# A third expert matrix for narrow last tiles: partial products on groups of PSUM's partitions, added by one more product

## The chip, the cores and the metric

The kernel runs on one core of one Trainium2 chip, as one launch. The metric is the device time in microseconds. Before the change three runs took 674.23 to 675.20 us, with a median of 675.03 us.

## What is computed

The reference is one layer over `x` of 64 sequences with 32 rows of 256 values (2048 rows, called tokens below), all in fp32: a cross attention on a context of 257 rows per sequence, a local attention, and a mixture of experts. The change is in the last of the three:

```python
def _L0_ffn_ref(hidden_states, Wr, br, W1, b1, W2, b2, W3, b3):
    x = hidden_states.reshape(-1, d)
    router_logits = x @ Wr + br
    expert_mask = jax.nn.one_hot(jnp.argmax(router_logits, axis=-1), num_experts, dtype=x.dtype)
    out = jnp.zeros_like(x)
    for e in range(num_experts):
        h = jax.nn.gelu(x @ W1[e] + b1[e], approximate=False)
        h = jax.nn.gelu(h @ W2[e] + b2[e], approximate=False)
        y = h @ W3[e] + b3[e]
        out = out + expert_mask[:, e:e + 1] * y
    return out.reshape(b, s, d)
...
x = x + _L0_xattn_ref(_layernorm(x, axis=-1), ctx_768, mask_BxS2_bf1, ...)
x = x + _L0_attn_ref(_layernorm(x, axis=-1), ...)
x = x + _L0_ffn_ref(_layernorm(x, axis=-1), ...)
```

There are 8 experts; W1 is 256x1024, W2 is 1024x512, W3 is 512x256. Each token goes to one expert, the one with the largest router logit.

## The kernel before

**Phases.** Until about 430 us the kernel does both attentions, 32 pairs of sequences one after another, and routes the tokens: it numbers the tokens of each expert in a table and writes their normed and plain rows to a table in DRAM (`table_x`). From then on the expert stage runs, in pieces.

**Pieces.** A piece is up to 256 tokens of one expert. Each expert has one piece of its own; for all but the first expert it is made of 128 tokens (half h=0) and the expert's last, partly filled tile (half h=1), which has 0, 32, 64, 96 or 128 rows. How many is known only on the chip: `quarters(i)` loads the number of steps of 32, and a `tc.Switch` with five cases runs `piece(j, P + 32 * case)`. Between two experts' pieces may stand a "between" piece of 128 tokens, in a `tc.If`, for experts with more than two tiles. So all the code for n = 128, 160, 192, 224 and 256 is there in each Switch, and the data choose.

**What a piece does.** `piece` (L1291) is a fixed order on TensorE: `first` (L1237, first matrix, 256 to 1024, gelu on ScalarE at L1243), `second` in three calls (L1253, second matrix, 1024 to 512, gelu at L1264 into `h2`), in their midst `turn_next` (transposes of the next piece's tokens, L1113, into `y_ps[1]`, copied out by ScalarE at L1116), then `third`. In `first` and `second` the weights are the operand that is loaded (128 columns of it) and the n tokens move through, so their time grows with n. In `third` it is the other way round: a block of `h2`, 128 x rows, is loaded and a block of W3, 128 x 256, moves through. It takes four such products (c = 0 to 3) to sum over the 512 rows of W3, all into the same part of a PSUM bank; a half of 32 rows therefore needs the four products that a half of 128 rows needs.

**The order around it.** The program's order is kept as written on TensorE, VectorE, ScalarE and GpSimd (POOL). In `third`, for each half: POOL adds the bias to the plain rows (`xb`, L1270), TensorE makes four products (L1273) into `y_ps[h]`, VectorE adds the two (`y`, L1277), and POOL scatters `y` to the output with an indirect DMA (L1278). POOL does the first half's scatter before the second half's `xb`. The block c=3 of `h2` is the last one that ScalarE writes (L1264), just after TensorE has ended the second matrix.

**Weights.** Three sets of buffers (`ring`) are refilled by four DMAs on SP's queue per expert, wa (L955), bo (L956), wb (L957) and wc (L961), in that order, each as soon as the last reader of its buffer is done. `bo` is read by POOL's `xb`.

**Constants.** `_COLS` names column ranges of one packed input, `pack2`. Its first part (up to `qhead`) comes with one DMA (L603), the rest with another (L606), between the first and the second half of the first context block.

**PSUM.** The eight banks have fixed roles in the expert stage: three for the first matrix, three for the second, `y_ps[0]` and `y_ps[1]` for the third matrix's two halves; `y_ps[1]` also takes the transposes.

Of the kernel before, what the change touches and what calls it, by code (L numbers as in the profile page):

```python
# [7 lines left out]
F32 = mybir.dt.float32  # L8
# [10 lines left out]
P = 128  # L19
# [3 lines left out]
B, S, D = 64, 32, 256  # L23
M, CD = 257, 192
HEADS, HD = 16, 16
E, F1, F2 = 8, 1024, 512
# [17 lines left out]
for _name, _w in (  # L44
    ("ident", 128),
    ("qhead", 2),
    ("ones", 128),
    ("before", 128),
    ("band", 128),
    ("own", 2),  # L50
    ("rank", E),
    ("step", NT - 1),
    ("tile", NT - 1),
    ("after", NT - 1),
    ("queue", E),
    ("queue_tile", E),
    ("quarter", 4),
    ("upto", E * E),
    ("row", P),
    ("column", E * NT),  # L60
    ("token", NT),
    ("here", 1),
):
    _COLS[_name] = (_n, _n + _w)
    _n += _w
# [12 lines left out]
def constants():  # L78

    import numpy as np  # L80

    c = np.zeros((P, NCONST), np.float32)
    p = np.arange(P)

    def put(name, value):
        a, b = _COLS[name]
        c[:, a:b] = value

    put("ident", p[:, None] == p[None, :])
    put("ones", 1.0)  # L90
    put("before", p[:, None] < p[None, :])
    near = (p[:, None] // S == p[None, :] // S) & (abs(p[:, None] - p[None, :]) <= 2)
    put("band", np.where(near, 0.0, FMAX))
    own = (p[:, None] // HD) % 2 == np.arange(2)[None, :]
    put("qhead", np.where(own, HD**-0.5, 0.0))
    put("own", np.where(own, -1.0, 0.0))
    put("rank", E - np.arange(E)[None, :])
    put("step", P * np.arange(1, NT)[None, :])
    put("tile", np.arange(NT - 1)[None, :])
    put("after", np.arange(1, NT)[None, :])  # L100
    put("queue", T * np.arange(E)[None, :])
    put("quarter", 32 * np.arange(4)[None, :])
    put("queue_tile", NT * np.arange(E)[None, :])
    put("upto", (np.arange(E)[:, None] >= np.arange(E)[None, :]).reshape(1, -1))
    put("row", p[None, :])
    put("column", P * np.arange(E * NT)[None, :])

    put("token", P * np.arange(NT)[None, :] + p[:, None] - T)
    put("here", p[:, None])
    return c  # L110


@with_exitstack
def perceiver_layer_kernel(
# [14 lines left out]
    nc = tc.nc  # L129
# [17 lines left out]
    k_ = {name: v2["consts"][:, a:b] for name, (a, b) in _COLS.items()}  # L147
# [40 lines left out]
    def bank(name, shape=(512,)):  # L188
        n = 1
        for w in shape:  # L190
            n *= w
        t = psp.tile([P, 512], F32, name=name, tag="bank")[:, 0:n]
        return t if len(shape) == 1 else t.rearrange("p (a b) -> p a b", b=shape[1])
# [365 lines left out]
    with tc.tile_pool(name="xq", bufs=1) as qpool, tc.tile_pool(  # L559
        name="xin", bufs=2  # L560
    ) as inp, tc.tile_pool(name="xkv", bufs=3) as kvp, tc.tile_pool(
        name="xp", bufs=2
# [261 lines left out]
        ps = bank("vl")  # L824
# [143 lines left out]
    rp = ctx.enter_context(tc.tile_pool(name="rp", bufs=1))  # L968
# [3 lines left out]
    h1 = rp.tile([P, F1 // P, 2 * P], F32, name="h1")  # L972
    h2 = rp.tile([P, F2 // P, 2 * P], F32, name="h2")
    xb_of = [rp.tile([P, D], F32, name=f"xb{i}") for i in range(2)]
    y_of = [rp.tile([P, D], F32, name=f"y{i}") for i in range(2)]

    def gather_rows(dst, at):
# [82 lines left out]
    f1_ps, f2_ps, y_ps = banks[0:3], banks[3:6], banks[6:8]  # L1060
# [12 lines left out]
    def buffer_of(j):  # L1073

        kind, i = order[j]
        if kind != "between":
            return i % 2 if i > 0 else 2
        return 2 if i < E - 1 else (i - E + 1) % 3  # L1080
# [19 lines left out]
    def tokens_of(j, h):  # L1100
        if order[j][0] == "early":
            return token0
        at = halves(j)[h]
        return token[:, at : at + 1]
# [160 lines left out]

    def third(j, n):
        _, _, wc, bo = ring[buffer_of(j)]
        for h, rows in enumerate((P, n - P) if n > P else (P,)):
            xt, xb, y = xt_of[h][j % 3], xb_of[h][0:rows, :], y_of[h][0:rows, :]
            nc.gpsimd.tensor_tensor(xb, xt[0:rows, 1, :], bo[0:rows, :], ALU.add)  # L1270
            ps = y_ps[h][0:rows, 0:D]
            for c in range(F2 // P):
                nc.tensor.matmul(  # L1273
                    ps, h2[:, c, h * P : h * P + rows], wc[:, c, :],
                    start=c == 0, stop=c == F2 // P - 1,
                )
            nc.vector.tensor_tensor(y, ps, xb, ALU.add)  # L1277
            nc.gpsimd.indirect_dma_start(  # L1278
                out=out[:, :],
                out_offset=bass.IndirectOffsetOnAxis(ap=tokens_of(j, h)[0:rows, :], axis=0),  # L1280
                in_=y,
                in_offset=None,
                bounds_check=T - 1,
                oob_is_err=False,
            )
# [5 lines left out]
    def piece(j, n):  # L1291
        first(j, n)
        second(j, n, (0, 1))
        turn_next(j)
        second(j, n, (2,))
        second(j, n, (3,))
        third(j, n)
# [36 lines left out]
    rest_2(tableT, pick)  # L1334
    gather(2, 1)
    third(0, P)
    gather(3, 0)
    first(1, P)
# [5 lines left out]
    second(1, P, (2,))  # L1344
    second(1, P, (3,))
    third(1, P)
    fetch_at(3)
    for i in range(1, E):
# [26 lines left out]
def laid_out(inputs):  # L1375
# [24 lines left out]
    def pack(*parts):  # L1400
# [5 lines left out]
        "mask": a["mask_BxS2_bf1"].view(np.uint8),  # L1406
        "pack1": pack(ct[:, :, :, M - 1], wk, np.concatenate([wv, wv], axis=0)),
        "pack2": pack(halves(a["L0_xattn_Wq"]), constants()),
        "pack3": pack(
            halves(a["L0_xattn_Wo"]), halves(a["L0_attn_Wq"].T),  # L1410
# [30 lines left out]
```

## Time and profile before

| | |
|---|---|
| median of 3 runs | 675.03 us (674.23 to 675.20) |
| the profiled execution | 675.32 us; the span of its instructions 673.5 us |
| granted TensorE clock | 0.989 of full speed over the span |
| expert stage | from about 433 us to the end |
| third matrix, 128x256, one multiply | 0.379 us from start to modelled end, x136 |
| the same with 32 or 64 columns loaded | x16 and x8 |
| last gelu of a piece with 160 rows (L1264) | 0.39 us |
| addition of y (L1277), 128x256 from PSUM | 0.425 us |
| bias addition xb on POOL (L1270) | 0.74 us |
| scatter on POOL (L1278) | 1.0 us |

How to read it: the profile is of one execution, so sums from its rows are held against its own 675.32 us. Times in the views are microseconds from the start of the span. PE is TensorE's multiply, PEld its weight load, which runs beside multiplies. An fp32 product shows as two loads and two multiplies. A multiply's end is modelled, and multiplies overlap in the pipeline: what a row of them costs is read from start to start, not from their durations. "128*32 128x256" is a multiply with 128 rows and 32 columns loaded and 256 columns moving. In brackets stands the engine's idle time before a group and what ended it; "issue" is a wait for nothing that the profile shows.

### The profile page before, as it was taken

How to read it: one execution, taken by the hardware profiler on the slowest of the kernel's cores; microseconds unless marked ns; L12 is line 12 of the kernel's file. 1: busy time of each engine (PE TensorE's matmuls, PEld its weight loads, DVE VectorE, ACT ScalarE, POOL GpSimd, SP SyncE). 2: the span in 40 equal slices, each digit the busy share in tenths (PEclk: the TensorE clock that was granted, in tenths of full speed). 3: DMA queues.
4: the chain of work that ended last, by engine and by line, in shares of the span. 5: the costliest groups of instructions: out<-in, count | busy, mean ns of one | idle time of the engine just before them, and what ended most of it. 6: DMA issues, size and time to landing. Idle time of an engine off the chain costs nothing.

```text
span 673.5 us, 18635 instructions
## 1 busy us (share of the span) xinstructions
PE 643.5 (96%) x7033; PEld 535.0 (79%) x7033; DVE 320.2 (48%) x1211; ACT 341.0 (51%) x1052; POOL 343.6 (51%) x725
## 2 busy tenths in 40 slices
PE   5999999999999999999999986899999999999994
PEld 3777777777777777877877875899999999989894
DVE  3485776777876877777786883610000000000000
ACT  2865775585684775766766644433323222243220
POOL 1596585687588588578587561222313122331120
PEclk9999999999999999999999998799999999999998
DMA  8932213303313322221200019464794627961000
GB/s 295 309 104 104 65 42 103 103 10 127 104 27 111 103 63 82 97 83 61 97 34 2 3 50 385 177 253 153 254 318 141 210 91 235 347 224 41 27 17 27
DMA packets 23094, 85.51 MB, mean 127 GB/s; under 512 B 2465, under 2 KB 7842, under 8 KB 20208
## 3 DMA queue, kind: packets, MB, share of 16 engines
q1 hardware_dynamic: 19984, 74.64, 31.9%
q0 software_dynamic: 2912, 8.65, 4.0%
q8 instruction: 72, 1.18, 0.7%
q14 instruction: 126, 1.03, 0.5%
HBM read 103.64 MB, written 6.56 MB: 164 GB/s over the span
## 4 chain that ended last, share of the span: by engine, by line
PE 88%; DVE 4%; DMA 3%; issue 2%; ACT 1%; POOL 1%; SPq 0%; ACTq 0%; POOLq 0%
PE moe L1253 17%; PE k L651 13%; PE v L668 12%; PE moe L1237 9%; PE t L750 8%; PE s L684 5%; PE moe L1273 5%; PE pv L769 4%; PE wo L799 2%; PE q L582 2%; PE av L372 2%; PE am L355 2%; DMA xt<-table_x,token 2%; DMA ct<-in_ctxt 1%; PE as L399 1%
## 5 line engine op out<-in xcount | busy, mean ns | idle before, releaser
L711 ACT ACTIVATE p<-p,nmx 128x256 f32<-128x256 f32 x256 | 127.2, 499 | 69.0 <-DVE nmx L706 68.1
L737 POOL TENSOR_SCALAR p<-p,rd 128x256 f32<-128x256 f32 x256 | 117.1, 478 | 84.1 <-DVE rd L734 30.3
L1253 PE MATMUL moe<-h,wb 128*128 128x128 f32 (+3 forms) x992 | 128.9, 289 | 0.3 <-issue 0.3
L1253 PEld LDWEIGHTS moe<-h,wb 128*128 128x128 f32 x992 | 124.1, 192 | 2.0 <-issue 0.4
L1277 DVE TENSOR_TENSOR y<-moe,xb 128x256 f32<-128x256 f32 (+2 forms) x20 | 8.5, 423 | 216.1 <-PE moe L1273 193.0
L706 DVE CUSTOM_DVE_ANT_0 p<-s,mb 128x256 f32<-128x256 f32 x256 | 108.0, 478 | 3.8 <-PE s L684 3.8
L651 PE MATMUL k<-cp,pack 64*128 64x512 f32 x384 | 95.3, 618 | 0.9 <-POOL cp L637 0.9
L756 DVE COPY pt<-t 128x512 f32<-128x512 f32 x114 | 72.6, 674 | 49.3 <-PE t L750 49.3
L668 PEld LDWEIGHTS v<-pack,cp 64*128 64x128 f32 x768 | 78.9, 187 | 19.1 <-issue 8.6
L637 POOL TENSOR_SCALAR cp<-ct,pack 128x256 f32<-128x256 f32 x189 | 87.6, 479 | 11.8 <-DMA ct<-in_ctxt 10.2
L668 PE MATMUL v<-pack,cp 64*128 64x256 f32 x768 | 90.9, 377 | 0.0
L1278 POOL DMA_INDIRECT out_x<-y,token x20 | 20.0, 1002 | 127.1 <-DVE y L1277 105.8
L1264 ACT ACTIVATE h<-moe,wa 128x128 f32<-128x128 f32 (+3 forms) x64 | 23.2, 380 | 101.8 <-PE moe L1253 96.3
L1243 ACT ACTIVATE h<-moe,wa 128x128 f32<-128x128 f32 (+3 forms) x120 | 38.6, 379 | 63.6 <-PE moe L1237 59.7
L1237 PEld LDWEIGHTS moe<-xT,wa 128*128 128x128 f32 x480 | 60.3, 191 | 7.2 <-issue 5.0
L651 PEld LDWEIGHTS k<-cp,pack 64*128 64x128 f32 x384 | 39.3, 191 | 33.6 <-issue 25.3
L1237 PE MATMUL moe<-xT,wa 128*128 128x128 f32 (+3 forms) x480 | 63.8, 291 | 1.8 <-ACT h L1243 1.0
L750 PE MATMUL t<-pack,p 128*128 128x128 f32 x512 | 64.5, 277 | 0.2
L750 PEld LDWEIGHTS t<-pack,p 128*128 128x128 f32 x512 | 55.6, 141 | 10.9 <-issue 5.6
L711 ACT ACTIVATION_READ_ACCUMULATOR p<-p,nmx 128x1 f32 x256 | 48.5, 189 | 0.0
L978 POOL DMA_INDIRECT xt<-table_x,token x24 | 25.1, 1044 | 45.2 <-PE moe L1253 23.1
L769 PEld LDWEIGHTS pv<-pt,v 128*32 128x32 f32 x2048 | 30.2, 110 | 12.6 <-issue 4.6
(197 smaller groups left out, 835.4 us busy)
## 6 DMA issues: line engine op xcount, KB each, us to landing
wb<-in_WB SPq DMA_DIRECT2D x17, 2048.0 KB
ct<-in_ctxt SPq DMA_DIRECT2D x15, 1542.0 KB
wa<-in_WA SPq DMA_DIRECT2D x17, 1030.0 KB
wc<-in_WC SPq DMA_DIRECT2D x17, 512.0 KB
table_x<-aw SPq DMA_DIRECT2D x8, 512.0 KB
bo<-in_b SPq DMA_DIRECT2D x17, 128.0 KB
m<-in_mask SPq DMA_DIRECT2D x16, 128.5 KB
ct<-in_ctxt SPq DMA_DIRECT2D x2, 771.0 KB
```

The source lines that it names most:

```text
L637: engine.tensor_scalar(cp[:, r, j, :], loaded[b // BG][0][:, r, b % BG, 0:KL], -1.0, clast[:, r, b : b + 1], ALU.mult, ALU.add,)
L651: nc.tensor.matmul(ps[c], wk[h, r, :], cp[h, r, :, :].rearrange("p b k -> p (b k)"), start=r == 0, stop=r == 2,)
L668: nc.tensor.matmul(ps[t][:, j * D : (j + 1) * D], cp[h, r, j, t * P : (t + 1) * P], wv[h, r, :], start=r == 0, stop=r == 2,)
L706: nc.vector.tensor_tensor_reduce(out=p[:, j, i, :], in0=ps[i][:, j * KL : (j + 1) * KL], in1=mb[:, b % BG, 0:KL], scale=1.0, scalar=mb[:, ...
L711: nc.scalar.activation(p[:, j, i, :], p[:, j, i, :], AF.Exp, bias=nmx[:, j, i : i + 1], scale=-1.0, accum_out=sums[:, j, i : i + 1],)
L737: nc.gpsimd.tensor_scalar(p[:, j, i, :], p[:, j, i, :], rd[:, j, i : i + 1], 1.0, ALU.mult, ALU.mult)
L750: nc.tensor.transpose(ps[:, i * P : (i + 1) * P], prob[n][:, j, i, t * P : (t + 1) * P], ident)
L756: nc.vector.tensor_copy(pT[n][:, j, t, :], ps)
L769: nc.tensor.matmul(pv[32 * i : 32 * i + 32, c, j, :], v[:, t, j, at : at + 32], pt[:, j, t, i * P + 64 * c : i * P + 64 * c + 64], start=t ...
L1237: nc.tensor.matmul(ps[:, i, 0:n], wa[:, at : at + P], x_j[:, c, 0:n], start=c == 0, stop=c == 1,)
L1243: nc.scalar.activation(h1[:, f + i, 0:n], ps[:, i, 0:n], AF.Gelu, bias=wa[:, at : at + 1])
L1253: nc.tensor.matmul(pss[f], wb[:, c, f * P : (f + 1) * P], h1[:, c, 0:n], start=c == 0, stop=c == F1 // P - 1,)
```

## The change

A constant with columns `sum32` (1 where the partition's number modulo 32 equals the column) and one `sum64` (modulo 64) are added to the pack, 96 columns in all, and a tile `parts` of 128 x 256. If the last tile has 32 or 64 rows (`few`), `third` does that half differently. Before the first half, the four products for it are made, each onto its own group of 32 of `y_ps[1]`'s partitions (four groups), or, with 64 rows, onto two groups of 64, with two products summed in each. VectorE copies all 128 partitions to `parts`. When the second half's turn comes, one product with `sum32` or `sum64` as the loaded operand adds the groups up, into the next 256 columns of the same bank. For a last tile of 96 or 128 rows, and for pieces of 128, nothing changes. POOL's and VectorE's other work keeps its order.

```diff
+    ("sum32", 32),
+    ("sum64", 64),
...
+    put("sum32", p[:, None] % 32 == np.arange(32)[None, :])
+    put("sum64", p[:, None] % 64 == np.arange(64)[None, :])
...
+    parts = rp.tile([P, D], F32, name="parts")
...
     def third(j, n):
         _, _, wc, bo = ring[buffer_of(j)]
+        few = n - P if P < n <= P + 64 else 0
+        if few:
+
+            wide = 32 if few <= 32 else 64
+            ps = y_ps[1][:, 0:D]
+            for c in range(F2 // P):
+                at = c * wide % P
+                nc.tensor.matmul(
+                    ps[at : at + few, :], h2[:, c, P:n], wc[:, c, :],
+                    start=c * wide < P, stop=(c + P // wide) >= F2 // P,
+                )
+            nc.vector.tensor_copy(parts, ps)
         for h, rows in enumerate((P, n - P) if n > P else (P,)):
             xt, xb, y = xt_of[h][j % 3], xb_of[h][0:rows, :], y_of[h][0:rows, :]
             nc.gpsimd.tensor_tensor(xb, xt[0:rows, 1, :], bo[0:rows, :], ALU.add)
-            ps = y_ps[h][0:rows, 0:D]
-            for c in range(F2 // P):
+            if h and few:
+                ps = y_ps[1][0:rows, D : 2 * D]
                 nc.tensor.matmul(
-                    ps, h2[:, c, h * P : h * P + rows], wc[:, c, :],
-                    start=c == 0, stop=c == F2 // P - 1,
+                    ps, k_["sum32" if wide == 32 else "sum64"][:, 0:few], parts,
+                    start=True, stop=True,
                 )
+            else:
+                ps = y_ps[h][0:rows, 0:D]
+                for c in range(F2 // P):
+                    nc.tensor.matmul(
+                        ps, h2[:, c, h * P : h * P + rows], wc[:, c, :],
+                        start=c == 0, stop=c == F2 // P - 1,
+                    )
             nc.vector.tensor_tensor(y, ps, xb, ALU.add)
```

## The prediction

> **What bounds the kernel now.** I read the page first, then the chain of waits over the expert stage, then the one source line that the change rewrites, then the timeline around the pieces that it touches. The page:
>
> ```profile
> PE 643.5 (96%) x7033; PEld 535.0 (79%) x7033; DVE 320.2 (48%) x1211; ACT 341.0 (51%) x1052; POOL 343.6 (51%) x725
> ...
> PE 88%; DVE 4%; DMA 3%; issue 2%; ACT 1%; POOL 1%; SPq 0%; ACTq 0%; POOLq 0%
> ```
>
> TensorE is busy for 96% and carries 88% of the chain. The change sits in the expert stage; the chain there, from 430 us on, by line:
>
> ```profile
> by line: PE moe L1253 47.7%; PE moe L1237 24.4%; PE moe L1273 12.9%; issue 5.5%; PE moe L1113 2.0%; PE moe L1027 1.3%; PE table_ps L549 0.7%; POOL xt L978 0.4%; POOL out_x L1278 0.4%; POOL xb L1270 0.3%; ACT h L1243 0.2%; PE moe L1205 0.1%;
> ```
>
> So TensorE time in this stage is kernel time, and L1273, the third matrix, is on the chain. The view of that source line says how often the change applies:
>
> ```profile
> L1273 PEld LDWEIGHTS moe<-wc,h x160: 106/190/193, 439.1 to 663.8; 128*128 128x128 f32 x136, 128*32 128x32 f32 x16, 128*64 128x64 f32 x8
> L1273 PE MATMUL moe<-wc,h x160: 378/379/463, 439.1 to 664.0; 128*128 128x256 f32 x136, 128*32 128x256 f32 x16, 128*64 128x256 f32 x8
> ```
>
> A product in fp32 is two load-and-multiply pairs, and a half takes four products, so 8 pairs. 16 pairs of 32 columns are two halves of 32 rows, 8 of 64 columns are one of 64 rows. Three pieces of the run change; the other thirteen take the old code. The timeline around the first of them (third starts at 493.91):
>
> ```profile
> 493.91 3.73 PE L1273 MATMUL moe<-wc,h 128*128 128x256 f32 x16
> 494.17 0.39 ACT L1264 ACTIVATE h<-moe,wa 128x160 f32<-128x160 f32 x1 [1.78 <-PE moe L1253]
> 495.73 1.43 PEld L1273 LDWEIGHTS moe<-wc,h 128*32 128x32 f32 x8 [0.33 <-issue]
> 495.90 0.42 DVE L1277 TENSOR_TENSOR y<-moe,xb 128x256 f32<-128x256 f32 x1 [14.79 <-PE moe L1273]
> 496.60 1.03 POOL L1278 DMA_INDIRECT out_x<-y,token  x1 [8.15 <-DVE y L1277]
> 497.66 0.74 POOL L1270 TENSOR_TENSOR xb<-xt,bo 32x256 f32<-32x256 f32 x1
> ```
>
> Note the second line: the last gelu of h2 ends at 494.56, 0.65 us after TensorE has gone on to the third matrix. Today nothing waits: the product that needs it is the fourth of h=0. TensorE alone, for this piece, the 64-row one, and the 128-row one (which has no narrow tile):
>
> ```profile
> 493.91 3.73 PE L1273 MATMUL moe<-wc,h 128*128 128x256 f32 x16
> 497.58 3.84 PE L1237 MATMUL moe<-xT,wa 128*128 128x128 f32 x32
> 501.25 3.74 PE L1253 MATMUL moe<-h,wb 128*128 128x128 f32 x32
> ...
> 556.66 3.76 PE L1273 MATMUL moe<-wc,h 128*128 128x256 f32 x16
> 560.35 3.84 PE L1237 MATMUL moe<-xT,wa 128*128 128x128 f32 x32
> 564.03 3.74 PE L1253 MATMUL moe<-h,wb 128*128 128x128 f32 x32
> ...
> 648.09 3.62 PE L1273 MATMUL moe<-wc,h 128*128 128x256 f32 x16
> 651.54 3.73 PE L1237 MATMUL moe<-xT,wa 128*128 128x128 f32 x32
> 655.12 3.74 PE L1253 MATMUL moe<-h,wb 128*128 128x128 f32 x32
> ```
>
> From 648.09 to 651.54 are 16 pairs: 0.216 us each, and a narrow half costs as many. From the start of third to the start of the second matrix after it: 7.03 us without narrow tiles, 7.34 with 32 columns, 7.37 with 64. So going into narrow tiles and out again costs 0.31 or 0.34 us today. Narrow windows split it: the last wide multiply starts at 495.42 and would be followed at 495.64; the narrow one comes at 495.73, plus its load (0.02): in, 0.11. Out, the rest, 0.20: 0.09 before the first wide load, 0.11 for that load, which nothing covers.
>
> **The change, part by part.** First the column groups. Do they run together? In the first phase:
>
> ```profile
> 36.38 1.25 PE L684 MATMUL s<-kt,qd 32*64 32x256 f32 x32
> 37.55 1.10 PE L769 MATMUL pv<-pt,v 128*32 128x64 f32 x64
> 38.59 2.85 PE L651 MATMUL k<-cp,pack 64*128 64x512 f32 x12
> ```
>
> L769 is the same form (32 columns, four partition groups of one PSUM bank): 64 multiplies in 1.04 us, 0.016 each. One after another they would need 0.06 each (0.112 at 128 columns moving and 0.216 at 256 give 0.0008 a column), 3.8 us. So four run at once, and I take that.
>
> The gain the change could have, then: 8 pairs in a row, 1.73 us, become 2 deep in 32-wide tiles (0.43), 4 deep in 64-wide ones (0.86). The Trainium skill (TensorEngine Tiling (Array Packing), "The Solution" and "Theoretical Speedup") promises up to 4x and 2x; by that alone 2 x 1.30 + 0.86 = 3.5 us come off. Against it the same page, "Key Properties": changing the tiling mode drains TensorE; it gives no price, the trace does, 0.31 to 0.34 us for in and out. And its "PSUM Bottleneck": faster products leave the copy out of PSUM as the limit. The rows decide these:
>
> 32-row piece, from 493.91. *In*: 0.11. Products 0 to 2 run at once, done 0.43 to 0.65 us later. Product 3 now comes ahead of h=0, and its weight load waits for the last gelu: it ends at 494.56, and TensorE takes up work 0.05 us after a gelu (narrow windows at 590: second gelu ends 590.63, the load that waited for it starts 590.68). So product 3 starts at 0.71 and ends, with its load of 0.02 and two multiplies, at 1.16. *Out*: 0.20. h=0's 8 pairs: 1.73. *In* again for the sum, since its left operand is 32 columns: 0.11. Two multiplies: 0.43. *Out*: 0.20. Sum 3.83. Today: 1.73 + 0.11 + 1.73 + 0.20 = 3.77. **+0.07** (before rounding), twice.
>
> 64-row piece: gelu ends at 557.34, so product 3 starts at 0.73 (products 0 and 2 share a tile and are done at about 1.0, side by side with it), ends at 1.21; out 0.20, 1.73, in 0.14, 0.43, out 0.20: 3.91 against 3.46 + 0.34 = 3.80: **+0.11**.
>
> Together +0.25 us. What the packing wins (1.30) goes to the sum product (0.43), the second pair of switches (0.31), and to waiting for a gelu that h=0 covers now (0.60 of 0.71).
>
> What I cost at nothing, and its cover:
> - The new VectorE copy (128x256 from PSUM; 0.425 us by the copies of that shape at L324 and L1002, bound 0.48 by L363). It can start at about 1.6 and the sum waits for it at 3.1; h=0's 1.73 us cover it, so the skill's PSUM limit does not bind. Without that cover it is 0.6 with its hand-overs. On VectorE it comes before both y additions; nothing else is queued there.
> - y of h=0 comes 1.4 us later, and with it, in POOL's order, its scatter (1.03), xb of h=1 (0.74), y of h=1 and its scatter. Behind them on SP's queue stand bo and wb of the expert after next, which wait for xb: 498.42 becomes 499.8; its first use is about 540, and no row shows TensorE waiting for a DMA in this stage. The next gather on POOL is at 509.55, the next writer of y_ps[1] L1113 at 504.83, y of h=1 ends near 500.2. Uncovered, each would cost up to 1.4.
> - The constants grow by 96 columns, 128 x 96 x 4 B = 49 KB, 0.16 us at the first slices' 300 GB/s, ahead of the second half of ctxt and the mask. The mask is waited for only by POOL (15.48); what TensorE needs of that is done near 19.4 and used at 22.3. Bound 0 to 0.16; I take 0.
> - TensorE's sequencer stops at a waiting load. At the sum it stops until the copy is done, about 495.9, and only then walks to the next piece: in the piece at 584 that took from 585.09 (end of the gelu it stood at) to 586.69, 1.6 us. So ready at 497.5; needed at 497.55 + 0.09 = 497.64. Just hidden; below it is a rival.
> - Six more multiplies and one copy per narrow branch move code. The chain shows "issue" of 4.3 us at 584.78, ScalarE coming late out of a branch; TensorE lost 1.4 there (0.35 + 1.05). That it moves is worth -1.4 to +1.4 us; I take 0.
>
> The profiled execution took 675.32 us (span 673.5 and 1.8 around it), the median of the runs is 675.03; nothing around the span changes, so I add 0.25 to the median: **675.3 us**.
>
> **Rivals.**
> (a) *The walk of the sequencer decides* (slower). Place: between the sum's load and the next piece, three times. Slack 0.1 us. Every 0.1 that copy plus hand-over or walk take beyond it is 0.3 us; past 0.4 over, the kernel is slower by over 0.2%. ScalarE's walk out of the same branch took 2.6 us; at that price it is +1.0 each, 678.3. For it: the slack is thin. Against: TensorE walked in 1.5 to 1.6 us at 494.66 and 585.1.
> (b) *The groups run one after another* (slower): 0.11 + 1.73 + 0.20 + 1.73 + 0.11 + 0.43 + 0.20 = 4.51, +0.74 each, 677.3. For: h=1 alone today gains nothing from 32 columns. Against: L769, L684.
> (c) *The gelu does not hold it* (faster): then product 3 ends at 0.55 to 0.6, -0.6 for 32 rows, -0.1 for 64: 673.8. Against: the load of product 3 reads h2.
> (d) *Code moves a stall*: 673.9 or 676.7.
>
> **How the numbers follow.** The forecast 0.69, spread 0.8 either way for my hand-overs and the runs' scatter (674.23 to 675.2): 674.5 to 676.1; (a) 0.12; (b) 0.04; (c) 0.07; (d) 0.08. A measurement here can tell about 0.2%, 1.35 us, from no change: 673.7 and 676.4. (c) and half of (d) fall at the lower bound: faster 0.05. (b), most of (a), half of (d): slower 0.15. Same 0.80. The range 673.9 to 676.8 leaves out the far ends of (a) and (b).
>
> **What would show it.** Right: L1273 rows of 32x256 in groups starting within 0.1 us; a gap on TensorE before product 3 until the gelu's end; h=0 from about 495.3; a copy ending near 495.8; the next L1237 about 497.64. Wrong: L1237 marked idle with "issue" after the sum (a); column multiplies 0.216 apart (b); no gap (c). The distance from third's start to the next L1253, 7.34 now, is the test: 7.41 by me, 8.1 by (b), 6.8 by (c).

## The result, and the profile after

Twenty runs of the changed kernel gave a median of 678.29 us (674.50 to 680.43), twenty of the kernel before, on the same chip, 675.45 us (671.22 to 677.18). The ratio is 1.0038, with a 95% interval of 1.0021 to 1.0054: slower by 0.38%, some 2.6 us (the medians differ by 2.84). The forecast was 675.3 us, no change. The profiled execution took 679.39 us (span 677.6), 4.1 us more than that of before.

First the page of the changed kernel: busy time of the engines, the granted TensorE clock in 40 slices, and the chain.

```profile
PE 647.4 (96%) x7039; PEld 536.1 (79%) x7039; DVE 321.5 (47%) x1214; ACT 340.8 (50%) x1052; POOL 343.5 (51%) x725
...
PEclk9998999999999999999999998799999998999998
...
PE 88%; DVE 4%; DMA 3%; issue 2%; ACT 1%; POOL 1%; SPq 0%; POOLq 0%; DVEq 0%
```

The clock row of before:

```profile
PEclk9999999999999999999999998799999999999998
```

Six more multiplies, three more operations on VectorE, the same shares within 1%: the page alone hides the loss. The clock row has two slices with an 8 that before had as 9. The one at 559 us (slice 33, counted from 0) lies in the expert stage. The timeline of TensorE leads there: the first piece with 32 rows, then the one with 64.

```profile
493.99 1.23 PE L1280 MATMUL moe<-wc,h 128*32 128x256 f32 x8
495.16 1.99 PE L1297 MATMUL moe<-wc,h 128*128 128x256 f32 x8
497.08 0.62 PE L1290 MATMUL moe<-parts,pack 128*32 128x256 f32 x2
497.63 3.84 PE L1242 MATMUL moe<-xT,wa 128*128 128x128 f32 x32
501.31 3.74 PE L1258 MATMUL moe<-h,wb 128*128 128x128 f32 x32
...
556.97 1.29 PE L1280 MATMUL moe<-wc,h 128*64 128x256 f32 x8
558.19 1.99 PE L1297 MATMUL moe<-wc,h 128*128 128x256 f32 x8
560.11 0.65 PE L1290 MATMUL moe<-parts,pack 128*64 128x256 f32 x2
560.69 1.60 PE L1242 MATMUL moe<-xT,wa 128*128 128x128 f32 x12
564.65 3.60 PE L1242 MATMUL moe<-xT,wa 128*128 128x128 f32 x20 [2.36 <-issue]
568.04 4.20 PE L1258 MATMUL moe<-h,wb 128*128 128x128 f32 x32
```

Lines L1280, L1297 and L1290 are the packed blocks, half h=0 and the sum. At 497.63 the next piece begins on time. At 560.69 it begins on time too, but after 12 of its 32 multiplies TensorE stands still for 2.36 us, and nothing that the profile shows is waited for. Such a stop is called a dry spot below. What follows is slower as well. The stretch from the start of that first matrix to the start of the second, after and then before (columns: length; busy time and number of instructions of PE, PEld, DVE, ACT and POOL; granted clock; busy share of DMA; GB/s):

```profile
560.69:568.04 7.35, 4.99 (x34) 4.91 (x33) 0.42 (x2) 1.87 (x6) 2.69 (x3) 0.83 0.63 210
```

```profile
560.35:564.03 3.68, 3.68 (x34) 3.68 (x34) 0.42 (x1) 1.87 (x6) 0.77 (x2) 1.00 0.82 246
```

The same work took 3.67 us longer: 2.36 of standing still, and 1.31 in which TensorE was busy longer, at a granted clock of 0.83 of full speed over that stretch instead of 1.00 (0.50 from 565.6 to 569.0). What TensorE lacked at 562 us is in the DMA's queues. Its code comes in packets of 16 KB on the queue q8: in the attention phase of the kernel before, one such packet came for every 256 instructions of TensorE (10,227 in the time of 40 packets), and the six dry spots of over 2 us in this study all ended 1.2 to 1.5 us after such a packet had landed. Below are the queues over 3.4 us from the instant at which TensorE's sequencer took the branch out of the 64-row piece (an instruction that the trace shows: 558.77 after, 557.44 before); columns: packets, MB, share of 16 engines. After:

```profile
q1 hardware_dynamic: 132, 0.97, 79.7%
q14 instruction: 1, 0.01, 0.6%
```

Before:

```profile
q1 hardware_dynamic: 88, 0.73, 70.0%
q8 instruction: 1, 0.02, 3.4%
q14 instruction: 1, 0.01, 0.6%
```

Before, TensorE's packet was under way 1.1 us after the branch (at 558.50). After, there is none in 3.4 us: it came at 562.23, 3.5 us after the branch, just as TensorE ran out of work (its 12th multiply ended at 562.29).

The pieces one by one, from the start of one first matrix to the start of the next, in us; `before_again` and `again` are second executions of the same two kernels on other chips:

| piece | before | before_again | after | again |
|---|---|---|---|---|
| 160 rows (32 in the last tile) | 17.00 | 17.00 | 17.18 | 18.17 |
| between | 13.04 | 13.11 | 13.14 | 13.14 |
| 160 rows (32) | 17.00 | 17.00 | 17.06 | 17.06 |
| between | 13.14 | 13.14 | 13.15 | 13.15 |
| 192 rows (64) | 19.59 | 19.59 | 19.71 | 19.71 |
| between, behind the 64-row tile | 13.10 | 13.03 | **17.25** | **15.77** |
| one expert's piece of 128 rows | 13.26 | 13.33 | 13.28 | 13.25 |
| between, at about 586 us | 14.46 | 16.92 | 13.14 | 13.15 |

The 18.17 of `again` is no dry spot: in that piece's first matrix TensorE waited 0.84 us for ScalarE, ahead of the packed blocks, and the kernels without the change show the like (18.00 in `const_only`, 17.98 in `code_untaken`).

Held against the span, before to after: the stage starts 0.25 earlier, the pieces up to the 64-row one sum to +0.59, then +4.15, +0.02 and -1.32, and +0.01 from there to the last piece; from the start of the last first matrix to the end of the span it is 22.87 instead of 22.00. That makes 4.1. The last +0.9 does not go with the change in every execution: from the start of the last third matrix to the end, the executions of this study took either 10.9 to 11.1 or 11.7 to 12.1, and `sum_free`, which has the changed kernel's instructions one for one, took 11.1, while `code_untaken`, which packs nothing, took 11.7. What decides between the two was not looked into.

### The profile page after: what moved, and what is told of

The parts are those of the page before. It is cut to its first block, busy times and chain, and to the rows that moved or that the text cites. A ratio compares the mean times of both kernels' runs of the same rounds, so it can differ in the third digit from the quotient of the medians.

```text
span 677.6 us, 18650 instructions
## 1 busy us (share of the span) xinstructions
PE 647.4 (96%) x7039; PEld 536.1 (79%) x7039; DVE 321.5 (47%) x1214; ACT 340.8 (50%) x1052; POOL 343.5 (51%) x725
## 4 chain that ended last, share of the span: by engine, by line
PE 88%; DVE 4%; DMA 3%; issue 2%; ACT 1%; POOL 1%; SPq 0%; POOLq 0%; DVEq 0%
PE moe L1258 17%; PE k L655 13%; PE v L672 12%; PE moe L1242 9%; PE t L754 8%; PE s L688 5%; PE pv L773 4%; PE moe L1297 4%; PE wo L803 2%; PE q L586 2%; PE av L376 2%; PE am L359 2%; DMA xt<-table_x,token 1%; DMA ct<-in_ctxt 1%; PE as L403 1%
## 5 line engine op out<-in xcount | busy, mean ns | idle before, releaser
L641 POOL TENSOR_SCALAR cp<-ct,pack 128x256 f32<-128x256 f32 x189 | 87.5, 479 | 11.7 <-DMA ct<-in_ctxt 10.1
L754 PEld LDWEIGHTS t<-pack,p 128*128 128x128 f32 x512 | 55.6, 141 | 10.9 <-issue 5.6
```

What stands on the lines that cost most here:

```text
L641: engine.tensor_scalar(cp[:, r, j, :], loaded[b // BG][0][:, r, b % BG, 0:KL], -1.0, clast[:, r, b : b + 1], ALU.mult, ALU.add,)
L754: nc.tensor.transpose(ps[:, i * P : (i + 1) * P], prob[n][:, j, i, t * P : (t + 1) * P], ident)
```

## The experiments

Three theories went in. **H** (hold): the sum's load waits on TensorE for VectorE's copy; while it waits the sequencer stands at it, so it leaves the branch later, and code of the next piece is asked for too late. **P** (place): the changed code is longer and lies elsewhere, and that alone moves a spot where code comes late. **S** (start): the larger constants delay the start, and the rest is scatter. Each ratio below is to the kernel before on the same chip, from 12 runs unless another number is given. One kernel's executions spread over about 6 us, so single spans are not compared; single rows are.

**The changed kernel once more** (`again`), with no edit.

> The changed kernel once more, for its scatter and a second trace. Three theories of the 2.8 us that it lost, of which 0.25 are its narrow pieces. H (hold): TensorE's sequencer stands at the sum's weight load until the copy is done (495.74 in place of 494.66), walks out of the branch 1.1 to 1.3 us later, and asks for the next piece's code that much later, so that TensorE runs dry in some executions, as at 562 for 2.4 us. P (place): the added instructions move all code behind them, and another place of the code gives other fetch stalls, whoever waits for what. S (start): the 49 KB more of constants delay the start. All three expect a ratio near 1.0038 to before; H expects the dry spots behind the three narrow pieces, P anywhere behind branches, S none, but a later expert stage.

678.61 us (674.50 to 680.37), ratio 1.0020 [1.0001, 1.0039]. The dry spot is again behind the 64-row piece, 2.50 us. The windows row of that first matrix:

```profile
561.71:567.90 6.19, 3.69 (x32) 3.61 (x32) 0.42 (x2) 1.75 (x6) 2.70 (x3) 1.00 0.66 192
```

Here the clock was 1.00 and the first matrix lost 2.51 us instead of 3.67: the dry spot belongs to the kernel; the lowered clock behind it came in five of the six executions that had a dry spot of over 2 us (0.50 for 3.4 us), and not in this one, whose dry spot was the longest.

**The sum without VectorE's copy** (`sum_free`): the added product reads weights in place of `parts`. Rows of narrow tiles are then not the layer's.

```diff
-    ps, k_["sum32" if wide == 32 else "sum64"][:, 0:few], parts,
+    ps, k_["sum32" if wide == 32 else "sum64"][:, 0:few], wc[:, 0, :],
```

> The changed kernel, but the sum product reads a block of the third matrix in place of the copied groups, so its rows of the narrow tiles are not the layer's. All instructions stay, in number and place; only the wait for the copy is gone, and the sequencer can walk on once the last gelu is done. H: a ratio of 1.000 to 1.001 (675.5 to 676), the first branch out of a narrow piece again near 0.1 us after the last gelu, no dry spot behind the narrow pieces. P and S: still 1.003 to 1.004.

678.73 us, ratio 1.0019 [0.9994, 1.0045]; dry spot of 2.48 us in the same place. This run did not do what it was made for. The copy reads the bank that the sum writes, so the sum still waited for it, and the branch still came late (in the first piece at 496.82, in `again` at 496.76). It says nothing on H.

**Code alone** (`code_untaken`): the kernel before, with TensorE code that never runs added to the case of 96 rows, so that TensorE's code is as much longer as in the changed kernel (3,584 bytes).

```diff
     def third(j, n):
         _, _, wc, bo = ring[buffer_of(j)]
+        if n == P + 96:
+            for _ in range(2):
+                ps = y_ps[1][:, 0:D]
+                nc.tensor.matmul(ps, h2[:, 0, 0:P], wc[:, 0, :], start=True, stop=True)
+                nc.vector.tensor_copy(parts, ps)
```

> The kernel before, with two products and two copies more in the case of 96 rows, which these data never take: TensorE's code grows by the same 3584 bytes as with the change, in the same seven branches, and nothing more runs. P: a ratio of 1.003 to 1.004, with stalls behind branches that differ from before's. H and S: 0.999 to 1.001.

677.58 us, ratio 1.0018 [0.9998, 1.0038]: by the time alone, undecided. By the trace, no dry spot behind the 64-row piece (13.20 us); the loss in the profiled execution is ScalarE coming late out of its branch at 586 us (16.91 us for that piece), which `before_again` shows as well. Length of code alone did not make the dry spot.

**Constants alone** (`const_only`): the kernel before with the 96 columns.

```diff
+    ("sum32", 32),
+    ("sum64", 64),
...
+    put("sum32", p[:, None] % 32 == np.arange(32)[None, :])
+    put("sum64", p[:, None] % 64 == np.arange(64)[None, :])
```

> The kernel before with the 96 columns of constants alone. S: 1.003, with the expert stage beginning about 2 us later. H and P: 0.999 to 1.001, the expert stage beginning within 0.2 us of before.

676.33 us, ratio 0.9993 [0.9973, 1.0012], and the first piece of the stage began at 439.0 us (440.9 in before), not 2 us later. S falls.

**The packing without the hold** (`hold_free`): the changed kernel with the copy moved behind everything else of `third`, and the sum reading weights, so that nothing on TensorE waits for VectorE. Rows of narrow tiles are not the layer's.

```diff
-            nc.vector.tensor_copy(parts, ps)
+            blocks = ps
...
-    ps, k_["sum32" if wide == 32 else "sum64"][:, 0:few], parts,
+    ps, k_["sum32" if wide == 32 else "sum64"][:, 0:few], wc[:, 0, :],
...
+        if few:
+            nc.vector.tensor_copy(parts, blocks)
```

> In the run that let the sum product read another tile, the sum still waited for VectorE, for its copy reads the same PSUM bank: the first branch out of a narrow piece stood at 496.82, 0.59 us after the first half's first product, as in the changed kernel. So it did not test H. Here the copy is moved behind everything in the third matrix, after the second y, and the sum reads a block of the third matrix (its rows of the narrow tiles are not the layer's). Nothing that TensorE does waits for it in the piece. All instructions stay in number. H: the branch out of the narrow piece comes about 1.1 us earlier, the dry spot of 2.4 us behind the 64-row piece goes or shrinks by 1.1 us or more, ratio to before 0.999 to 1.001. P: the dry spot stays, 1.002 to 1.004.

676.31 us, ratio 1.0002 [0.9972, 1.0031]. TensorE behind the 64-row piece:

```profile
556.42 0.65 PE L1290 MATMUL moe<-wc,pack 128*64 128x256 f32 x2
557.00 4.08 PE L1242 MATMUL moe<-xT,wa 128*128 128x128 f32 x32
560.91 1.28 PE L1258 MATMUL moe<-h,wb 128*128 128x128 f32 x10
```

All 32 multiplies follow one another, in 4.08 us (3.84 before). The queues over 3.4 us from the branch (553.98) have TensorE's packet again:

```profile
q1 hardware_dynamic: 91, 0.75, 61.6%
q8 instruction: 1, 0.02, 2.9%
q14 instruction: 1, 0.01, 0.8%
```

The three narrow pieces took 17.07, 17.06 and 19.71 us, as in the changed kernel. So packing, mode switches, the wait for the gelu and the sum are all still there, and only the hold, and with it the dry spot, is gone.

**The hold without the packing, first try** (`hold_only`): the kernel before; five copies on VectorE at the start of `third`, and behind the narrow half one product of 8 columns that reads what they wrote. By mistake this kernel also had five steps instead of three in the normalisation's loop on POOL.

```diff
+        if P < n <= P + 64:
+            for _ in range(5):
+                nc.vector.tensor_copy(parts[:, 0:n], h2[:, 3, 0:n])
...
+            if h and rows <= 64:
+                nc.tensor.matmul(
+                    y_ps[1][0:rows, D : D + 8], h2[:, 0, P:n], parts[:, 0:8],
+                    start=True, stop=True,
+                )
...
-            for _ in range(3):
+            for _ in range(5):
```

> The kernel before with the hold alone: the narrow half's four products stay as they were, one after another, and behind them stands one small product (8 columns) that reads a tile which five VectorE copies in a row fill, the first of them waiting for the last gelu; it writes columns that nobody reads. So TensorE's sequencer stands there until about 1.1 us later than before, with TensorE's own work longer by less than 0.1 us per narrow piece, and TensorE's code has the changed kernel's size. H: a dry spot behind the 64-row piece as in the changed kernel, near 2.4 us, ratio 1.002 to 1.004. P: no dry spot there, as in the run with code in the case not taken, which had the same code size; 1.000 to 1.002.

689.01 us (6 runs), ratio 1.0187 [1.0145, 1.0228]. The two further steps put the stage's first multiply of `first` at 451.2 us instead of 440.9, so this ratio says nothing on the hold. The trace does: a dry spot of 2.39 us behind the 64-row piece (17.09 us for the piece that follows).

**The blocks added by VectorE** (`dve_sum`): the changed kernel without copy and sum on TensorE; VectorE adds the groups from PSUM, 0.42 us each. Nothing on TensorE waits for it.

```diff
-            nc.vector.tensor_copy(parts, ps)
...
-                ps = y_ps[1][0:rows, D : 2 * D]
-                nc.tensor.matmul(
-                    ps, k_["sum32" if wide == 32 else "sum64"][:, 0:few], parts,
-                    start=True, stop=True,
-                )
+                for at in range(wide, P, wide):
+                    nc.vector.tensor_tensor(xb, y_ps[1][at : at + rows, 0:D], xb, ALU.add)
+                ps = y_ps[1][0:rows, 0:D]
```

> A version meant to beat both: the blocks on PSUM's partition groups as in the change, but no copy and no sum product; VectorE adds the groups to xb one by one (three additions of 0.42 us for 32 rows, one for 64), off TensorE's path. By the trace, a narrow piece's third matrix then costs TensorE 0.71 + 0.45 + 0.20 + 1.73 + 0.20 or less, 3.1 in place of 3.77 us, so 0.6 to 0.7 us off each of three pieces, 2.0 in all, and the sequencer is held by nothing after the last gelu. H: 0.997 (673 to 674.5), no dry spot behind the narrow pieces. P: the gain of 2 us less or plus what the place of the code gives, 0.995 to 1.001.

672.79 us (670.26 to 676.73), ratio 0.9953 [0.9924, 0.9983]: faster than the kernel before. The narrow pieces took 16.42, 16.42 and 19.04 us, 0.58, 0.58 and 0.55 less than before; no dry spot.

**The changed kernel with its code moved** (`shifted`): 24 products in the first such expert's case of 96 rows, which never runs; all later code of TensorE lies further back.

```diff
+        if j == 2 and n == P + 96:
+            for _ in range(24):
+                nc.tensor.matmul(
+                    y_ps[1][:, 0:D], h2[:, 0, 0:P], wc[:, 0, :], start=True, stop=True
+                )
```

> The changed kernel with 24 products more in the first expert's case of 96 rows, which these data never take: all TensorE code behind it moves by 96 instructions. H: the dry spot behind the 64-row piece stays within 0.5 us of 2.4, ratio near 1.003. P: it goes, or others come elsewhere; anything from 0.998 to 1.006.

678.48 us, ratio 1.0047 [1.0019, 1.0076]. The dry spot left its place: it is now behind the second piece with 32 rows, and the 64-row piece is followed without one.

```profile
527.11 0.62 PE L1295 MATMUL moe<-parts,pack 128*32 128x256 f32 x2
527.66 1.72 PE L1242 MATMUL moe<-xT,wa 128*128 128x128 f32 x13
531.61 3.38 PE L1242 MATMUL moe<-xT,wa 128*128 128x128 f32 x19 [2.24 <-issue]
```

H had let me expect it to stay. The place of the code does matter after all, but as to where, not whether: a second condition that goes with the hold.

**The hold without the packing, mended** (`hold_alone`): `hold_only` without the mistake.

> The run with the hold alone carried two more Newton steps in the norms by a mistake (64 more POOL instructions, the expert stage beginning 10 us later), so its ratio of 1.0187 says nothing; its trace had the dry spot of 2.4 us at the same place behind the 64-row piece. The same kernel without that mistake: narrow products as before, then one small product that waits for five VectorE copies. H: ratio 1.002 to 1.005, the dry spot behind the 64-row piece, and no instruction fetch of TensorE's within 1.5 us of the branch out of it. P: 1.000 to 1.002 as with the code in the case not taken.

679.58 us, ratio 1.0041 [1.0010, 1.0072]. TensorE behind the 64-row piece, L1277 the third matrix unpacked, L1282 the product that waits:

```profile
560.08 3.76 PE L1277 MATMUL moe<-wc,h 128*128 128x256 f32 x16
563.68 0.23 PE L1282 MATMUL moe<-parts,h 128*64 128x8 f32 x2
563.84 1.60 PE L1238 MATMUL moe<-xT,wa 128*128 128x128 f32 x12
567.74 3.90 PE L1238 MATMUL moe<-xT,wa 128*128 128x128 f32 x20 [2.29 <-issue]
```

No packing, no sum, and the same picture: 12 multiplies, then 2.29 us dry. TensorE's packet came at 565.14, 2.9 us after the branch at 562.29. The hold alone brings the dry spot. The ratio holds more than that: in the profiled execution the first piece with 32 rows took 20.90 us (17.00 before), because TensorE waited 1.92 us for a late ScalarE in its first matrix, before that piece's hold, and the clock fell behind it.

**Moved code without the hold** (`shifted_free`): `hold_free` with the edit of `shifted`; rows of narrow tiles are not the layer's.

> With all code behind the first expert moved by 96 instructions, the changed kernel's dry spot went from behind the 64-row piece to behind the second 32-row piece, as long (2.2 us). So the place of the code decides which held piece runs dry. Here the same shift with the copy behind everything, so that nothing holds the sequencer (the narrow rows of the sum are not the layer's). H: no dry spot behind any narrow piece, 0.999 to 1.001. If place alone decided: the dry spot stays where it was in the shifted run, 1.003 to 1.005.

675.97 us, ratio 1.0002 [0.9977, 1.0027]. Behind the second piece with 32 rows, where `shifted` ran dry:

```profile
526.23 0.62 PE L1295 MATMUL moe<-wc,pack 128*32 128x256 f32 x2
526.78 3.84 PE L1242 MATMUL moe<-xT,wa 128*128 128x128 f32 x32
530.46 3.74 PE L1258 MATMUL moe<-h,wb 128*128 128x128 f32 x32
```

In both places of the code, then, the dry spot is there with the hold and gone without it.

**The blocks behind half h=0** (`blocks_last`): `dve_sum` with the packed products in the second half's turn, so that h=0's products cover the last gelu.

```diff
-        if few:
-
-            wide = 32 if few <= 32 else 64
-            ps = y_ps[1][:, 0:D]
-            for c in range(F2 // P):
...
+        wide = 32 if few <= 32 else 64
...
             if h and few:
+                for c in range(F2 // P):
+                    at = c * wide % P
+                    nc.tensor.matmul(
+                        y_ps[1][at : at + few, 0:D], h2[:, c, P:n], wc[:, c, :],
+                        start=c * wide < P, stop=(c + P // wide) >= F2 // P,
+                    )
```

> The version with VectorE's additions, but with the blocks behind the first half's products and not ahead of them. Then the last gelu is covered by the first half, as in the kernel before, and a narrow piece's third matrix costs TensorE 1.73 + 0.11 + 0.43 + 0.20 = 2.5 us (0.86 in place of 0.43 with 64 rows: 2.9) against 3.77: 1.3, 1.3 and 0.9 off, 3.5 in all, 671.8. The forecast's third term, the gelu that the first half no longer covers, is then worth 0.6 per 32-row piece against the version with the blocks first. If the wait for the gelu were not the cost, it would time as that version does, 0.995. H: branch out as early as in before, no dry spot; but TensorE needs the next code 1.2 us sooner, so a dry spot of up to 0.5 us may appear. Ratio 0.993 to 0.996.

672.94 us (668.74 to 675.01), ratio 0.9949 [0.9922, 0.9976]. The end of the second piece with 32 rows, L1291 being h=0 and L1281 the four packed products:

```profile
523.93 1.89 PE L1291 MATMUL moe<-wc,h 128*128 128x256 f32 x8
525.75 0.64 PE L1281 MATMUL moe<-wc,h 128*32 128x256 f32 x8
526.32 3.84 PE L1242 MATMUL moe<-xT,wa 128*128 128x128 f32 x32
```

From h=0's start to the next piece are 2.39 us, before 3.67: the piece took 15.73 us (17.00 before), the 64-row one 18.73 (19.59). The first 32-row piece took 16.77, with 0.77 of waiting for ScalarE in its first matrix. From `dve_sum` it can't be told apart by the runs: these two pieces gain another 0.3 and 0.7 us, and 0.26 of that is lost behind the 64-row piece to "issue". Both versions beat the kernel before by more than the noise; the changed kernel had ratios above 1.

**The kernel before once more** (`before_again`), one execution for its rows.

> The kernel before once more, for a second trace of it: how much of a single profile's difference is scatter. Expected: the narrow pieces at 17.00, 17.0 and 19.6 us again, no dry spot behind them, while the start, the spots of lower TensorE clock and ScalarE's late branches vary by 1 to 4 us.

675.94 us. The narrow pieces are those of the first execution (17.00, 17.00, 19.59), and ScalarE's late branch at 586 us cost more, 16.92 us for that piece.

Side by side:

| kernel | TensorE waits for VectorE in the third matrix | dry spot (us), behind which tile | ratio to before |
|---|---|---|---|
| changed, first / again | yes | 2.36 / 2.50, 64 rows | 1.0038 / 1.0020 |
| `sum_free` | yes | 2.48, 64 rows | 1.0019 |
| `shifted` | yes | 2.24, second of 32 rows | 1.0047 |
| `hold_alone` (no packing) | yes | 2.29, 64 rows | 1.0041 |
| `hold_free` | no | none | 1.0002 |
| `shifted_free` | no | none | 1.0002 |
| `code_untaken`, `const_only` (no packing) | no | none | 1.0018, 0.9993 |
| `dve_sum` | no | none | 0.9953 |
| `blocks_last` | no | none (0.26) | 0.9949 |

## Why the prediction was wrong

**What held.** The prices of the edit itself. Forecast +0.07, +0.07 and +0.11 us for the three pieces; measured +0.18, +0.06 and +0.12. (Of the +0.18, 0.12 lay in that piece's first matrix, 4.54 us instead of 4.42, ahead of the third; `hold_free` has 17.07.) The groups run at once: eight multiplies took from 493.99 to 495.16 with a wait inside, and in `blocks_last`, where they wait for nothing, the next product began 0.57 after the first of them; one after another they would take 1.73. That ends rival (b). The wait for the gelu is there, on the load of the fourth block:

```profile
493.99 0.15 PEld L1280 LDWEIGHTS moe<-wc,h 128*32 128x32 f32 x6 [0.17 <-issue]
494.16 0.39 ACT L1269 ACTIVATE h<-moe,wa 128x160 f32<-128x160 f32 x1 [1.78 <-PE moe L1258]
494.61 0.14 PEld L1280 LDWEIGHTS moe<-wc,h 128*32 128x32 f32 x2 [0.46 <-ACT h L1269]
495.16 1.99 PE L1297 MATMUL moe<-wc,h 128*128 128x256 f32 x8
495.26 0.42 DVE L1284 COPY parts<-moe 128x256 f32<-128x256 f32 x1 [14.31 <-PE moe L1280]
```

The load starts 0.06 us after the gelu's end, which ends rival (c). (The terms of (c), 1.3 us in all, give 674.0 from the forecast, not 673.8.) The price of that wait shows when it is taken away: from `dve_sum` to `blocks_last` the 32-row piece falls from 16.42 to 15.73 us, by 0.69, where 0.60 had been reckoned (the two versions also order the switches differently). The copy ended at 495.68 and the sum began at 497.08, so it was covered. The constants cost nothing that can be measured. From third's start to the next second matrix, 7.34 before, are 7.32 after from the first block's own start at 493.99 (the forecast's 7.41 counted from 0.11 earlier, with the switch in; so counted they are 7.43): not 8.1 and not 6.8.

**What failed.** The step "TensorE's sequencer stops at a waiting load ... Just hidden", in the list of what was costed at nothing. Its own sum was right: the forecast had the sequencer ready at 497.5, the next piece needed at 497.64, and it began at 497.63. The error was to follow the sequencer only to the first instruction of the next piece. The code behind that instruction has to be brought in, and that was late as well: a term that the forecast put at nothing and that cost 2.36 us. In the three pieces the branch came 1.1, 1.2 and 1.3 us later than before (495.7, 525.9 and 558.8; before 494.7, 524.7 and 557.4, in executions whose pieces differ by up to 0.3). TensorE's next 16 KB packet came later by far more: 4.9, 3.3 and 3.5 us after the branch, where before it was 1.1, 1.0 and 1.1.

What came between is a refill of weights. SP issues the DMA of `wa`, 1.05 MB, as soon as the last gelu is done, which the hold does not delay. Behind the 64-row piece, after and then before:

```profile
557.58 0.35 SPq L959 DMA_DIRECT2D wa<-in_WA  x1
```

```profile
557.37 0.35 SPq L955 DMA_DIRECT2D wa<-in_WA  x1
```

Its packets began 0.97 us later, at 558.55 and 558.34. Before, TensorE had branched at 557.44, and its code packet came at 558.50, with 12 of `wa`'s 128 rows begun. After, TensorE branched only at 558.77, when `wa` was already on its way, and the code packet came at 562.23, as `wa`'s last packets ended. The traces on record agree: in all 18 narrow pieces with the hold (six executions), `wa` began 0.2 to 0.5 us ahead of the branch, and the code packet came with at least 127 of the 128 rows begun, in 17 of them within 0.3 us of `wa`'s end and in one 0.6 ahead of it. In all 24 without the hold (eight executions), `wa` began 0.9 us behind the branch, and the packet came 1.0 to 2.5 us after the branch, with 7 to 42 rows begun. So with a hold of 1.2 us the code packet came behind a transfer of 3.7 us instead of at its beginning. That the refill is what made it wait is read from this order; no run moved the refill.

In two of the pieces the code that was already in lasted until then; behind the 64-row piece it ended after 12 multiplies. The stop cost 2.36 us, and, where the clock fell behind it, 1.3 more in the first matrix and 0.5 in what followed (4.15 for the whole piece; 2.67 in `again`).

Rival (a), the slower one, named the right place and the wrong mechanism: it priced the walk out of the branch, three times 1.0, and the walk cost nothing (each piece began on time). What occurred is one dry spot of 2.2 to 2.5 us in a piece that had begun on time. Its total, 678.3, is close to the 678.29 measured only by accident. Rival (d), moved code, is half of the truth: `shifted` shows that the place of the code decides behind which of the held pieces TensorE runs dry; `code_untaken`, `hold_free` and `shifted_free` show that without the hold it does not.

**Part of the loss came back.** In the piece at about 586 us ScalarE comes late out of its branch in many executions. In the nine executions without a dry spot of over 2 us behind the 64-row piece, that piece took 13.91 to 16.92 us; in the five with one, 13.14 to 13.61. That fits a median that moved by less than the dry spot and the slow clock together. Why ScalarE is in time when TensorE is late was only seen, not tested.

**What stays open.** How the refill holds the code packet up: no trace shows when the packet was asked for, so whether it stood behind `wa`'s packets in a queue or was itself asked for late can't be told; once it appears it takes 1.04 us (1.82 before). A run that delays the refill beyond the branch would test it. Open too is how the place of the code decides which held piece runs dry, for the packet was late behind all 18 and only one piece in each execution ran dry; that fixed packets of code reach less far into one piece than into another would fit, and is only argued.

## What to carry to other kernels

When an instruction near the end of a branch waits on the engine that sets the time, follow its sequencer beyond the first instruction of what comes next: look in the DMA queues for when the code packets behind the branch come, which large transfers are issued ahead of them, and how long the code already in will last. The wait itself may be hidden and the stop comes microseconds later, marked "issue", in a piece that the change doesn't touch. And products packed on groups of PSUM's partitions paid here once the groups were added off TensorE (-0.5%) and put where other products cover the last activation, since the 1.3 us that packing frees are otherwise spent on the sum, its mode switches and the wait.

## What was not expected of the hardware

- A branch that TensorE reached over 1 us late, 0.2 to 0.5 us after a weight refill of 1.05 MB had begun, was followed by its next code packet 2.8 to 4.9 us after it instead of 1.0 to 2.5, and in one piece of three by 2.2 to 2.5 us without work.
- After such a stop of 2.36 us the granted clock over 7.35 us was 0.83 in one execution; after one of 2.50 us in another it was 1.00 over 6.19 us. Stops of the same kind had two prices.
- Executions of one kernel spread by about 6 us (671.22 to 677.18), with ScalarE late out of branches (idle with "issue" for 3.6 us at one place in `before`, 5.8 in `before_again`) and spots of low clock (0.7 to 0.8 in slice 3 of some pages) moving from one to the next: effects of 1 us are to be read from rows, not from runs.
